# A graph network's prologue: load order, a broadcast by TensorE, sums on other engines, and the moved row counts of later pairs

## The chip, the cores and the metric

The kernel runs on one core of a Trainium2 chip. The metric is the device time of one launch in microseconds (us), the median of several runs. One profiled execution of each kernel gives the spans and traces quoted here. All timed runs that are compared were in the fast state; most experiments were timed once only, with no state on record, so there the traces are compared and not the times. Runs that share a chip are compared with each other first.

## The reference, cut to what matters

128 independent graphs of 128 nodes go through two layers. Layer 0 is graph attention with 8 heads. Layer 1 is two hypergraph convolutions with a layer norm between them.

```python
x, adj: (128, 128, 512), (128, 128, 128)           # float32
# layer 0
feats = einsum('bnf,hfu->bhnu', X, W)              # W: 8 heads, 512 -> 64
dense = leaky_relu(e_self[:, :, :, None] + e_neigh[:, :, None, :], 0.2) + NEG_BIG * (1 - A)
out   = einsum('bhij,bhju->bhiu', softmax(dense), feats) + b
x     = layernorm(x + relu(out))
# layer 1
h = relu(hypergraph_conv(x, adj, W1, b1))          # 512 -> 1024
h = layer_norm(h, gamma, beta)
y = hypergraph_conv(h, adj, W2, b2)                # 1024 -> 512
x = layernorm(x + (y + x))
```

All weights are shared by the graphs. The kernel therefore prepares them once, in its prologue. The layer norm between the two convolutions is folded into W2: each row is scaled by gamma, and a row of weighted means is subtracted (`gw`). A second such row (`bw`) carries beta.

## The kernel before: the parts that matter here

Graphs are handled in 64 pairs, in a software pipeline. Every step of every pair has a number, the list is sorted by it, and the steps are emitted in that order. The numbers order the instructions on each engine; they are no times. The large products with the weights (features, hidden, output) are done by a seven-product scheme, which needs sums of weight blocks (`second_sums`, `prepare_hidden`).

```python
    # first loads: W0 in four blocks on SyncE's queue, then
    as_bc = everywhere(a_self, F, "as_bc")     # everywhere: broadcast load on ScalarE's queue
    an_bc = everywhere(a_neigh, F, "an_bc")
    load(0)                                    # adjacency and its first row, SyncE
    load_blocks(0, nc.scalar)                  # pair 0's x, for the transposes
    load_edges(0, nc.scalar)
    b0_bc = everywhere(b0, F, "b0_bc")
    b2_bc = everywhere(b2, F, "b2_bc")
    for t, ap in ((b1_sb, b1), (gb[:, 0, :], gamma), (gb[:, 1, :], beta)):
        nc.scalar.dma_start(t, ap.rearrange("(k p) -> p k", p=P))
    # ... cut ...
    def nodes(p, s):                           # node degrees of a pair, ends in one small tile
        # ... cut: VectorE, w <- (a != 0) * w with two SBUF inputs ...
        s["dr"] = work.tile([P, B], F32, tag="dr", name=f"dr_{p}")   # a single buffer
        nc.vector.transpose(s["dr"], dn)
    def write_nodes(p, s):
        nc.sync.dma_start(s["dd"].rearrange("b c n -> (b c) n"), s["dr"])
    # ... cut ...
    def prepare_output_sums():                 # pv: the means, made by 32 matmuls
        for j in range(2):
            nc.vector.tensor_copy(sums[:, j * QU:(j + 1) * QU], pv[j][:2, :QU])
        nc.sync.dma_start(sums_d, sums)        # to DRAM ...
        for c, t in ((0, gw), (1, bw_bc)):     # ... and back into all partitions
            nc.sync.dma_start(t, sums_d[c].partition_broadcast(P))
    def prepare_output_blocks(some):           # 16 scalings of W2 by gamma, minus gw
        # ... cut ...
                nc.vector.scalar_tensor_tensor(
                    blk[:, k, :], blk[:, k, :], gb[:, 0, c:c + 1], gw[:, j * QU:(j + 1) * QU],
                    op0=ALU.mult, op1=ALU.subtract,
                )
    # ... cut ...
    first = {                                  # places of the first pairs' steps
        ("nodes", 0): 15.0, ("write_nodes", 0): 16.5, ("spread_nodes", 0): 18.5,
        # ... cut ...
        ("nodes", 1): 17.6, ("write_nodes", 1): 17.9, ("x_transpose", 1): 14.5,
        # ... cut ...
    }
```

Names used below: **pf** is the first layer's feature product, **nb** the neighbour rows on which masks, leaky relu, row maxima (**nm**) and exponentials work, **pav** the attend product, **pv** the means, **pz** the propagate product, **ph** the hidden product in seven parts (accumulators phX, phY, phW), **py** the output product. **y** is a pair's output of the first layer (at L824 of the second), **eT** the transposed exponentials, **dr** the small tile with a pair's node degrees, **ab** its edge blocks. TensorE is called cold where its matmuls take about double the time, warm otherwise.

Of the kernel before, what the change touches and what calls it, by code (L numbers as in the profile page):

```python
# [20 lines left out]
def kernel(  # L21
# [45 lines left out]
    nc = tc.nc  # L67
# [21 lines left out]
    def bank(name):  # L89
        return psum.tile([P, HALF], F32, tag="bank", name=name)  # L90
# [13 lines left out]
    def load_blocks(p, queue=None):  # L104
        s = st[p]
        gs = slice(2 * p, 2 * p + 2)

        s["xb"] = work.tile([P, 2 * NB, P], F32, tag="xb", name=f"xb_{p}")
        rows = x[gs].rearrange("g (b n) (f c) -> f n (g b) c", b=NB, f=NB)
        for f in range(NB):  # L110
            (queue or nc.sync).dma_start(s["xb"][f * B:(f + 1) * B], rows[f])

    def load_edges(p, queue=None):
        s = st[p]

        s["ab"] = work.tile([P, 2 * NB, B], F32, tag="ab", name=f"ab_{p}")
        rows = adj[2 * p:2 * p + 2].rearrange("g (b n) (f e) -> f n (g b) e", b=NB, f=NB)
        for f in range(NB):
            (queue or nc.sync).dma_start(s["ab"][f * B:(f + 1) * B], rows[f])
# [22 lines left out]
    def everywhere(ap, n, name):  # L142
        t = const.tile([P, n], F32, name=name)
        nc.scalar.dma_start(t, ap.partition_broadcast(P))
        return t

    as_bc = everywhere(a_self, F, "as_bc")
    an_bc = everywhere(a_neigh, F, "an_bc")
    load(0)
    load_blocks(0, nc.scalar)  # L150
    load_edges(0, nc.scalar)
    b0_bc = everywhere(b0, F, "b0_bc")
    b2_bc = everywhere(b2, F, "b2_bc")
    bw_bc = const.tile([P, F], F32, name="bw_bc")
# [3 lines left out]
    for t, ap in ((b1_sb, b1), (gb[:, 0, :], gamma), (gb[:, 1, :], beta)):  # L158
        nc.scalar.dma_start(t, ap.rearrange("(k p) -> p k", p=P))
# [28 lines left out]
    def second_sums(w, b12, some=slice(0, 4)):  # L188

        b11, b21, b22, t4, t1, t2, t3 = (w[i] for i in range(7))  # L190
        for dst, in0, in1 in ((t1, b12, b11), (t2, b22, t1), (t3, b22, b12), (t4, b21, t2))[some]:
            nc.vector.tensor_tensor(dst, in0, in1, op=ALU.subtract)
# [13 lines left out]
    def prepare_first_sums():  # L206
        second_sums([w0_sb[:, i] for i in range(7)], w0_12)

    def prepare_hidden(i):
        a11, a12, a22, s1, s2, s3, s4 = (w1_sb[:, i] for i in range(7))  # L210
        dst, in0, in1, op = (
            (s1, w1_21, a22, ALU.add), (s2, s1, a11, ALU.subtract), (s3, a11, w1_21, ALU.subtract),
            (s4, a12, s2, ALU.subtract),
        )[i]
        nc.vector.tensor_tensor(dst, in0, in1, op=op)
# [4 lines left out]
    def prepare_output():  # L220
# [3 lines left out]
        nc.vector.tensor_copy(gbs[:, :, 1], gb[:, 1, :])  # L224
        pv = made["pv"] = [bank(f"pv{j}") for j in range(2)]
# [7 lines left out]
    def prepare_output_sums():  # L233
        pv = made["pv"]
        sums = const.tile([2, F], F32, name="sums")
        for j in range(2):
            nc.vector.tensor_copy(sums[:, j * QU:(j + 1) * QU], pv[j][:2, :QU])
        sums_d = dram.tile([2, F], F32, tag="sums_d", name="sums_d")
        nc.sync.dma_start(sums_d, sums)
        gw = work.tile([P, F], F32, tag="y2", name="gw")  # L240
        for c, t in ((0, gw), (1, bw_bc)):
            nc.sync.dma_start(t, sums_d[c].partition_broadcast(P))
        made["gw"] = gw
# [11 lines left out]
    def prepare_output_block_sums(some):  # L255
        second_sums([w2_sb[:, i, :, :QU] for i in range(7)], w2_12, some)
# [613 lines left out]
    def o_norm(p, s):  # L870
# [9 lines left out]
        (15.8, load_weights, (w2_blocks, w2t, DH // 2, QU)),  # L880
        (16.0, load_weights, (w1_blocks[:2], w1t, F // 2, HALF)),
        (80.2, load_weights, (w1_blocks[2:], w1t, F // 2, HALF)),
        (103.0, prepare_output, ()), (116.5, prepare_output_sums, ()),
        (112.0, prepare_hidden, (0,)), (112.5, prepare_hidden, (1,)),
        (114.5, prepare_hidden, (2,)), (115.0, prepare_hidden, (3,)),
        (122.4, prepare_output_blocks, (slice(0, 2),)),
        (128.4, prepare_output_blocks, (slice(2, 4),)),
        (130.6, prepare_output_block_sums, (slice(0, 2),)),
        (132.8, prepare_output_block_sums, (slice(2, 4),)),
# [4 lines left out]
        ("nodes", 0): 15.0, ("write_nodes", 0): 16.5, ("spread_nodes", 0): 18.5,  # L894
        ("x_transpose", 0): 11.5, ("edges", 0): 15.2, ("scale_edges", 0): 15.4,
        ("spread_rows", 0): 13.5, ("neighbours", 0): 14.0, ("load_rows", 0): 14.2,
        ("propagator", 0): 103.5, ("r_evict", 0): 104.0,
        ("nodes", 1): 17.6, ("write_nodes", 1): 17.9, ("x_transpose", 1): 14.5,
        ("edges", 1): 110.4, ("scale_edges", 1): 110.5,
        ("spread_rows", 1): 79.9, ("neighbours", 1): 80.0,  # L900
        ("propagator", 1): 117.7, ("r_evict", 1): 118.0,
# [10 lines left out]
    for p in range(PAIRS):  # L912
        if p > 1:
            todo.append((p * T, load, (p,)))
            todo.append((p * T + 19.0, load_blocks, (p,)))
            todo.append((p * T + 28.5, load_edges, (p,)))
        for lag, time, name, since, fn, args in steps:
# [11 lines left out]
            todo.append((first.get((name, p), (p + lag) * T + time), run, (fn, p, args)))  # L929
# [46 lines left out]
```

## Time and profile before

| | before |
|---|---|
| median of 3 runs | 2587.31 us (2584.8 to 2587.83) |
| span of the profiled run | 2586.4 us |
| TensorE busy | 2515.8 us |
| TensorE idle before 120 us | 53 us |
| attend of pair 1 begins (the landmark) | 117.71 us |

A line of a timeline gives the start and the length in us, the engine, the source line, the operation with output and inputs, the shapes, and how many instructions were merged. In brackets stands how long the engine had idled before it, and what ended the idling by the profile's account. The lines are in the prediction.

### The profile page before, as it was taken

The numbers are of one execution on the slowest core, as the hardware profiler recorded it, in microseconds if no ns is written. First come the engines' busy times: TensorE is split into PE (matmuls) and PEld (weight loads), VectorE is DVE, ScalarE is ACT, GpSimd is POOL, SyncE is SP. The second block draws the span as 40 slices with busy tenths as digits, with TensorE's granted clock in tenths as the row PEclk, the third lists the DMA queues.
The fourth block names the chain that finished last, engine by engine and source line by source line (L and its number), as shares of the span: only waits on it lengthen the run. The fifth ranks groups of instructions, "written<-read, shape, count | busy, mean of one in ns | idle before, by whom it ended". The sixth has DMA issues, their size and how long they took to land.

```text
span 2586.4 us, 48239 instructions
## 1 busy us (share of the span) xinstructions
PE 2515.8 (97%) x16312; PEld 2274.8 (88%) x16312; DVE 2146.5 (83%) x4650; ACT 1514.4 (59%) x4293; POOL 1714.1 (66%) x1797
## 2 busy tenths in 40 slices
PE   4799999999999999999999999999999999999997
PEld 3699899899999999989899999999989998999996
DVE  4788888888888888888888888888888888888875
ACT  2365565565565565565565665665665665665662
POOL 1567667667667667667667667667667667667753
PEclk8899999999999999999999999999999999999999
DMA  5444444444444444444444444444444444444430
GB/s 146 116 135 132 143 136 132 143 137 132 142 138 132 142 138 132 145 135 132 135 139 137 137 139 136 136 142 134 135 141 137 134 143 135 134 141 137 135 118 33
DMA packets 428250, 345.57 MB, mean 134 GB/s; under 512 B 146658, under 2 KB 377058, under 8 KB 428004
## 3 DMA queue, kind: packets, MB, share of 16 engines
q1 hardware_dynamic: 422132, 340.77, 44.5%
q10 hardware_dynamic: 5872, 1.72, 0.4%
q8 instruction: 130, 2.13, 0.3%
q14 instruction: 116, 0.95, 0.1%
HBM read 240.66 MB, written 101.72 MB: 132 GB/s over the span
## 4 chain that ended last, share of the span: by engine, by line
PE 89%; DMA 4%; DVE 3%; issue 2%; POOL 2%; SPq 0%; ACT 0%; ACTq 0%; POOLq 0%; DVEq 0%
PE phX L725 17%; PE pyX L417 14%; PE phW L725 9%; PE pfX L417 8%; PE pyW L417 8%; PE pav L599 8%; PE phY L725 4%; PE pz L690 4%; PE pq L849 4%; PE pfW L417 4%; PE pyY L417 4%; PE pfY L417 2%; DMA nb<-rd 1%; PE pd L373 1%; DMA dnb<-dd_d 1%
## 5 line engine op out<-in xcount | busy, mean ns | idle before, releaser
L519 POOL TENSOR_TENSOR nb<-nb,neg 128x512 f32<-128x512 f32 x256 | 320.0, 1272 | 117.9 <-DMA nb<-rd 75.0
L725 PEld LDWEIGHTS phX<-zS,w_sb 128*128 128x128 f32 x3072 | 364.8, 193 | 37.5 <-issue 37.5
L293 ACT COPY py<-pyX 128x257 f32<-128x257 f32 (+1 forms) x192 | 71.7, 374 | 548.0 <-PE pyX L417 548.0
L725 PE MATMUL phX<-zS,w_sb 128*128 128x128 f32 x3072 | 376.0, 276 | 7.1 <-issue 7.1
L776 POOL TENSOR_TENSOR sq<-sq 128x512 f32<-128x512 f32 (+2 forms) x384 | 344.9, 898 | 32.4 <-ACT sq L765 11.3
L526 ACT ACTIVATE nb<-nb,ft 128x128 f32<-128x128 f32 x1024 | 325.2, 389 | 50.1 <-POOL nb L519 48.0
L540 ACT ACTIVATE nb<-nb,nm 128x128 f32<-128x128 f32 x1024 | 320.2, 392 | 17.9 <-DVE nm L532 17.9
L646 POOL TENSOR_TENSOR rso<-veo,mhalf 128x2 f32<-128x2 f32 x64 | 44.8, 700 | 344.3 <-DVE veo L644 302.6
L630 DVE SCALAR_TENSOR_TENSOR y<-y,x 128x512 f32<-128x512 f32 x128 | 155.6, 1216 | 137.9 <-POOL y L623 137.9
L599 PEld LDWEIGHTS pav<-ft,eT 128*128 128x128 f32 x2048 | 251.4, 194 | 11.8 <-issue 2.6
L755 ACT ACTIVATE h<-h,b_sb 128x128 f32<-128x128 f32 x768 | 242.1, 392 | 16.9 <-DVE h L740 16.9
L417 PE MATMUL pyX<-w_sb,hS 128*128 128x257 f32 (+1 forms) x1024 | 248.1, 384 | 2.2 <-DVE hS L399 1.8
L599 PE MATMUL pav<-ft,eT 128*128 128x65 f32 x2048 | 246.5, 274 | 2.5 <-DVE eT L561 1.9
L417 PE MATMUL pyW<-w_sb,hS 128*128 128x256 f32 x1024 | 244.1, 380 | 3.7 <-DVE y L808 3.2
L417 PE MATMUL pyX<-w_sb,h 128*128 128x257 f32 (+1 forms) x1024 | 243.2, 379 | 0.0
L623 POOL TENSOR_TENSOR y<-y,b_bc 128x512 f32<-128x512 f32 x128 | 162.1, 1266 | 95.1 <-DVE y L614 95.1
L417 PEld LDWEIGHTS pyW<-w_sb,hS 128*128 128x128 f32 x1024 | 192.1, 189 | 37.2 <-DVE y L808 10.2
L417 PEld LDWEIGHTS pyX<-w_sb,hS 128*128 128x128 f32 x1024 | 190.2, 191 | 28.0 <-issue 2.1
L417 PEld LDWEIGHTS pyX<-w_sb,h 128*128 128x128 f32 x1024 | 189.3, 190 | 24.9
L399 POOL TENSOR_TENSOR xS<-xT 128x256 f32<-128x256 f32 x124 | 117.9, 951 | 89.5 <-DVE xT L337 89.5
L532 DVE TENSOR_REDUCE nm<-nb 128x4 f32<-128x512 f32 x256 | 173.6, 679 | 0.4 <-ACT nb L526 0.4
L293 ACT COPY ph<-phX 128x512 f32<-128x512 f32 x192 | 112.3, 585 | 97.0 <-PE phX L725 93.8
(127 smaller groups left out, 5843.2 us busy)
## 6 DMA issues: line engine op xcount, KB each, us to landing
nb<-rd SPq DMA_DIRECT2D x128, 512.0 KB, 5.9
ed<-nb SPq DMA_DIRECT2D x126, 512.0 KB, 3.2
eb<-ed SPq DMA_DIRECT2D x504, 128.0 KB, 2.9
x<-in_x_dram SPq DMA_DIRECT2D x64, 512.0 KB, 6.9
out_dram<-o SPq DMA_DIRECT2D x64, 512.0 KB, 2.8
xb<-in_x_dram SPq DMA_DIRECT2D x252, 128.0 KB, 3.0
a<-in_adj_dram SPq DMA_DIRECT2D x64, 128.0 KB, 6.1
w<-in_adj_dram SPq DMA_DIRECT2D x128, 64.0 KB, 3.9
```

Source lines behind the costliest of these rows:

```text
L293: nc.scalar.copy(t[:, :n], s[kind, "X"][:, :n])
L417: nc.tensor.matmul(to[:, :n], lhs[:, k, :], rhs[:, k, :n], start=bool(start) and k == 0, stop=(k == nk - 1), skip_group_check=True,)
L519: nc.gpsimd.tensor_tensor(t, t, neg[:, :, None, :].to_broadcast([P, NB, HH, B]), op=ALU.add)
L526: nc.scalar.activation(t, t, AF.Prelu, bias=s["ft"][:, g, h, 0:1], alpha=SLOPE)
L532: nc.vector.tensor_reduce(s["nm"][:, g, hs], scores(p, s, g, hs).rearrange("p b h j -> p h b j"), AX.XY, ALU.max, negate=True,)
L540: nc.scalar.activation(t, t, AF.Exp, bias=s["nm"][:, g, h:h + 1])
L599: nc.tensor.matmul(t[:, h * (U + 1):(h + 1) * (U + 1)], s["eT"][:, g, q * HH + h, :], s["ft"][:, g, q * HH + h, 2:], start=True, stop=True,)
L623: nc.gpsimd.tensor_tensor(s["y"][:, g, :], s["y"][:, g, :], b0_bc, op=ALU.add)
L630: nc.vector.scalar_tensor_tensor(y, y, 0.0, s["x"][:, g, :], op0=ALU.max, op1=ALU.add)
L725: nc.tensor.matmul(to[:, m * N:(m + 1) * N], w[:, k, m * P:(m + 1) * P], rhs[:, k, :], start=bool(start) and m == 0 and k == 0, stop=(k == ...
L755: nc.scalar.activation(dst[:, k, :], src[:, k, :], AF.Relu, bias=b1_sb[:, c:c + 1])
L776: nc.gpsimd.tensor_tensor(t[:, :n, :], t[:, :n, :], t[:, n:2 * n, :], op=ALU.add)
```

## The change

The intent is to shorten the prologue: fewer waits ahead of the first matmul, weights earlier, the means without a trip through DRAM, some sums on GpSimd and ScalarE, and the node counts of later pairs at other places.

```diff
-    as_bc = everywhere(a_self, F, "as_bc")        # b0, b2, b1, gamma, beta follow on ScalarE's queue
-    load(0)
-    load_blocks(0, nc.scalar)
-    load_edges(0, nc.scalar)
+    everywhere(as_bc, a_self, nc.scalar)
+    everywhere(an_bc, a_neigh, nc.scalar)
+    load_blocks(0)                                # on SyncE's queue, ahead of the adjacency
+    load(0)
+    load_edges(0)
+    def load_vectors(some):                       # gamma, beta, b0 / b1, b2: later, on SyncE's queue
 ... cut ...
-            nc.vector.tensor_copy(sums[:, j * QU:(j + 1) * QU], pv[j][:2, :QU])
-        nc.sync.dma_start(sums_d, sums)
-        for c, t in ((0, gw), (1, bw_bc)):
-            nc.sync.dma_start(t, sums_d[c].partition_broadcast(P))
+            nc.scalar.copy(made["sums"][:, j * QU:(j + 1) * QU], made["pv"][j][:2, :QU])
+    def prepare_output_spread():                  # gw and bw stay in PSUM banks
+            nc.tensor.matmul(made[n], made["sel"][:, c, :], made["sums"], start=True, stop=True)
+    def prepare_output_bias():
+        nc.scalar.copy(bw_bc, made["bw"])
 ... cut ...
-        (15.8, load_weights, (w2_blocks, w2t, DH // 2, QU)),
-        (16.0, load_weights, (w1_blocks[:2], w1t, F // 2, HALF)),
-        (80.2, load_weights, (w1_blocks[2:], w1t, F // 2, HALF)),
-        (103.0, prepare_output, ()), (116.5, prepare_output_sums, ()),
+        (15.75, load_vectors, (0,)), (15.8, load_weights, (w1_blocks, w1t, F // 2, HALF)),
+        (16.0, load_weights, (w2_blocks, w2t, DH // 2, QU)), (16.1, load_vectors, (1,)),
+        (79.1, prepare_hidden, (nc.gpsimd, 0)), (79.2, prepare_hidden, (nc.gpsimd, 1)),
+        (80.0, prepare_output_vectors, ()), (98.0, prepare_output, ()),
 ... cut ...
+        (122.0, prepare_output_blocks, (slice(2, 4),)),
+        (126.5, prepare_output_block_sums, (nc.gpsimd, slice(0, 2))),
 ... cut ...
-        ("nodes", 0): 15.0, ("write_nodes", 0): 16.5, ("spread_nodes", 0): 18.5,
+        ("nodes", 0): 14.45, ("write_nodes", 0): 14.5, ("spread_nodes", 0): 15.9,
+        ("attend", 0): 97.85, ("attended", 0): 99.7,           # all four groups ahead of the means
-        ("nodes", 1): 17.6, ("write_nodes", 1): 17.9,
+        ("nodes", 1): 79.92, ("write_nodes", 1): 80.15,
+        ("nodes", 2): 130.0, ("write_nodes", 2): 130.1, ("nodes", 3): 150.0,
```

More of the change, by code (lines that the diff above doesn't have):

```diff
@@ L102, in load, with load_blocks @@
             nc.sync.dma_start(s["w"][:, g, :], adj[2 * p + g, 0, :].partition_broadcast(P))
-    def load_blocks(p, queue=None):
+    def load_blocks(p):
         s = st[p]
@@ L110, in load_blocks, with load_edges @@
         for f in range(NB):
-            (queue or nc.sync).dma_start(s["xb"][f * B:(f + 1) * B], rows[f])
-    def load_edges(p, queue=None):
+            nc.sync.dma_start(s["xb"][f * B:(f + 1) * B], rows[f])
+    def load_edges(p):
         s = st[p]
@@ L118, in load_edges @@
         for f in range(NB):
-            (queue or nc.sync).dma_start(s["ab"][f * B:(f + 1) * B], rows[f])
+            nc.sync.dma_start(s["ab"][f * B:(f + 1) * B], rows[f])
     def block(dst, ap, i, j, rows, cols):
@@ L140, with everywhere @@
         w0_blocks.append((dst, raw.rearrange("p k (h u) -> p k h u", h=HH), j))
-    def everywhere(ap, n, name):
-        t = const.tile([P, n], F32, name=name)
-        nc.scalar.dma_start(t, ap.partition_broadcast(P))
-        return t
-    as_bc = everywhere(a_self, F, "as_bc")
-    an_bc = everywhere(a_neigh, F, "an_bc")
-    load(0)
-    load_blocks(0, nc.scalar)
-    load_edges(0, nc.scalar)
-    b0_bc = everywhere(b0, F, "b0_bc")
-    b2_bc = everywhere(b2, F, "b2_bc")
-    bw_bc = const.tile([P, F], F32, name="bw_bc")
+    def everywhere(t, ap, queue):
+        queue.dma_start(t, ap.partition_broadcast(P))
+    as_bc, an_bc, b0_bc, b2_bc, bw_bc = (
+        const.tile([P, F], F32, name=n) for n in ("as_bc", "an_bc", "b0_bc", "b2_bc", "bw_bc")
+    )
     b1_sb = const.tile([P, KH], F32, name="b1_sb")
     gb = const.tile([P, 2, KH], F32, name="gb")
-    for t, ap in ((b1_sb, b1), (gb[:, 0, :], gamma), (gb[:, 1, :], beta)):
-        nc.scalar.dma_start(t, ap.rearrange("(k p) -> p k", p=P))
+    everywhere(as_bc, a_self, nc.scalar)
[4 more added lines that the diff above has]
+    def load_vectors(some):
+        queue = nc.sync
+        if some == 0:
+            for t, ap in ((gb[:, 0, :], gamma), (gb[:, 1, :], beta)):
+                queue.dma_start(t, ap.rearrange("(k p) -> p k", p=P))
+            everywhere(b0_bc, b0, queue)
+        else:
+            queue.dma_start(b1_sb, b1.rearrange("(k p) -> p k", p=P))
+            everywhere(b2_bc, b2, queue)
     w2_sb = const.tile([P, 7, KH // 2, QU + 1], F32, name="w2_sb")
@@ L186, with second_sums @@
     nc.gpsimd.memset(dn, 0.0)
-    def second_sums(w, b12, some=slice(0, 4)):
+    def second_sums(engine, w, b12, some=slice(0, 4)):
         b11, b21, b22, t4, t1, t2, t3 = (w[i] for i in range(7))
         for dst, in0, in1 in ((t1, b12, b11), (t2, b22, t1), (t3, b22, b12), (t4, b21, t2))[some]:
-            nc.vector.tensor_tensor(dst, in0, in1, op=ALU.subtract)
+            engine.tensor_tensor(dst, in0, in1, op=ALU.subtract)
     def prepare_first(half):
@@ L206, in prepare_first_sums, with prepare_hidden @@
     def prepare_first_sums():
-        second_sums([w0_sb[:, i] for i in range(7)], w0_12)
-    def prepare_hidden(i):
+        second_sums(nc.vector, [w0_sb[:, i] for i in range(7)], w0_12)
+    def prepare_hidden(engine, i):
         a11, a12, a22, s1, s2, s3, s4 = (w1_sb[:, i] for i in range(7))
@@ L214, in prepare_hidden, with prepare_output_vectors, prepare_output @@
         )[i]
-        nc.vector.tensor_tensor(dst, in0, in1, op=op)
+        engine.tensor_tensor(dst, in0, in1, op=op)
     gbs = const.tile([P, KH, 2], F32, name="gbs")
     made = {}
-    def prepare_output():
+    def prepare_output_vectors():
         nc.vector.tensor_scalar(gbs[:, :, 0], gb[:, 0, :], 1.0 / DH, None, op0=ALU.mult)
         nc.vector.tensor_copy(gbs[:, :, 1], gb[:, 1, :])
+        made["sel"] = work.tile([2, 2, P], F32, tag="y2", name="sel")
+        nc.gpsimd.tensor_copy(
+            made["sel"], ident[:2, :2].unsqueeze(2).to_broadcast([2, 2, P])
+        )
+    def prepare_output():
         pv = made["pv"] = [bank(f"pv{j}") for j in range(2)]
@@ L233, in prepare_output_sums @@
     def prepare_output_sums():
-        pv = made["pv"]
-        sums = const.tile([2, F], F32, name="sums")
+        made["sums"] = const.tile([2, F], F32, name="sums")
         for j in range(2):
-            nc.vector.tensor_copy(sums[:, j * QU:(j + 1) * QU], pv[j][:2, :QU])
-        sums_d = dram.tile([2, F], F32, tag="sums_d", name="sums_d")
-        nc.sync.dma_start(sums_d, sums)
-        gw = work.tile([P, F], F32, tag="y2", name="gw")
-        for c, t in ((0, gw), (1, bw_bc)):
-            nc.sync.dma_start(t, sums_d[c].partition_broadcast(P))
-        made["gw"] = gw
+            nc.scalar.copy(made["sums"][:, j * QU:(j + 1) * QU], made["pv"][j][:2, :QU])
+    def prepare_output_spread():
+        made["gw"], made["bw"] = (bank(n) for n in ("gw", "bw"))
+        for c, n in enumerate(("gw", "bw")):
+            nc.tensor.matmul(
+                made[n], made["sel"][:, c, :], made["sums"], start=True, stop=True
+            )
+    def prepare_output_bias():
+        nc.scalar.copy(bw_bc, made["bw"])
     def prepare_output_blocks(some):
@@ L253, in prepare_output_blocks, with prepare_output_block_sums @@
                 )
-    def prepare_output_block_sums(some):
-        second_sums([w2_sb[:, i, :, :QU] for i in range(7)], w2_12, some)
+    def prepare_output_block_sums(engine, some):
+        second_sums(engine, [w2_sb[:, i, :, :QU] for i in range(7)], w2_12, some)
     def prepare_mean_columns():
@@ L879 @@
         (11.8, load_blocks, (1,)), (15.65, load, (1,)), (15.7, load_edges, (1,)),
-        (15.8, load_weights, (w2_blocks, w2t, DH // 2, QU)),
-        (16.0, load_weights, (w1_blocks[:2], w1t, F // 2, HALF)),
-        (80.2, load_weights, (w1_blocks[2:], w1t, F // 2, HALF)),
-        (103.0, prepare_output, ()), (116.5, prepare_output_sums, ()),
-        (112.0, prepare_hidden, (0,)), (112.5, prepare_hidden, (1,)),
-        (114.5, prepare_hidden, (2,)), (115.0, prepare_hidden, (3,)),
-        (122.4, prepare_output_blocks, (slice(0, 2),)),
-        (128.4, prepare_output_blocks, (slice(2, 4),)),
-        (130.6, prepare_output_block_sums, (slice(0, 2),)),
-        (132.8, prepare_output_block_sums, (slice(2, 4),)),
+        (15.75, load_vectors, (0,)), (15.8, load_weights, (w1_blocks, w1t, F // 2, HALF)),
+        (16.0, load_weights, (w2_blocks, w2t, DH // 2, QU)), (16.1, load_vectors, (1,)),
+        (79.1, prepare_hidden, (nc.gpsimd, 0)), (79.2, prepare_hidden, (nc.gpsimd, 1)),
+        (80.0, prepare_output_vectors, ()), (98.0, prepare_output, ()),
+        (112.1, prepare_output_sums, ()), (117.75, prepare_output_spread, ()),
+        (110.6, prepare_hidden, (nc.vector, 2)), (110.7, prepare_hidden, (nc.vector, 3)),
+        (119.85, prepare_output_bias, ()),
+        (117.8, prepare_output_blocks, (slice(0, 1),)),
+        (118.1, prepare_output_blocks, (slice(1, 2),)),
+        (122.0, prepare_output_blocks, (slice(2, 4),)),
+        (126.5, prepare_output_block_sums, (nc.gpsimd, slice(0, 2))),
+        (132.0, prepare_output_block_sums, (nc.vector, slice(2, 4))),
         (100.0, prepare_mean_columns, ()),
@@ L893 @@
     first = {
-        ("nodes", 0): 15.0, ("write_nodes", 0): 16.5, ("spread_nodes", 0): 18.5,
+        ("nodes", 0): 14.45, ("write_nodes", 0): 14.5, ("spread_nodes", 0): 15.9,
         ("x_transpose", 0): 11.5, ("edges", 0): 15.2, ("scale_edges", 0): 15.4,
         ("spread_rows", 0): 13.5, ("neighbours", 0): 14.0, ("load_rows", 0): 14.2,
-        ("propagator", 0): 103.5, ("r_evict", 0): 104.0,
-        ("nodes", 1): 17.6, ("write_nodes", 1): 17.9, ("x_transpose", 1): 14.5,
-        ("edges", 1): 110.4, ("scale_edges", 1): 110.5,
-        ("spread_rows", 1): 79.9, ("neighbours", 1): 80.0,
-        ("propagator", 1): 117.7, ("r_evict", 1): 118.0,
+        ("attend", 0): 97.85, ("attended", 0): 99.7, ("propagator", 0): 97.9, ("r_evict", 0): 100.0,
+        ("nodes", 1): 79.92, ("write_nodes", 1): 80.15, ("x_transpose", 1): 14.4,
+        ("edges", 1): 110.4, ("scale_edges", 1): 110.5, ("spread_nodes", 1): 101.0,
+        ("spread_rows", 1): 79.9, ("neighbours", 1): 80.1,
+        ("propagator", 1): 117.76, ("r_evict", 1): 121.8,
+        ("leaky", 1, 0, 0): 117.85, ("leaky", 1, 0, 1): 117.9, ("leaky", 1, 1, 0): 119.9,
+        ("largest", 1, 0, 0): 118.0, ("largest", 1, 0, 1): 118.2, ("largest", 1, 1, 0): 120.2,
+        ("masked", 1, 0, 0): 109.0,
+        ("nodes", 2): 130.0, ("write_nodes", 2): 130.1, ("nodes", 3): 150.0,
+        ("write_nodes", 3): 150.1, ("skip", 0): 128.5,
     }
@@ L913 @@
         if p > 1:
-            todo.append((p * T, load, (p,)))
+            todo.append(({2: 81.0, 3: 131.0}.get(p, p * T), load, (p,)))
             todo.append((p * T + 19.0, load_blocks, (p,)))
@@ L928 @@
                 }.get((name,) + args[:1], time)
-            todo.append((first.get((name, p), (p + lag) * T + time), run, (fn, p, args)))
+            time += (p + lag) * T
+            todo.append((
+                first.get((name, p) + args, first.get((name, p), time)), run, (fn, p, args)
+            ))
     with tc.manual_schedule():
```

## The prediction

> **What bounds the kernel now.** I read the page's busy shares first. They say TensorE, and the row after it shows VectorE well below.
>
> ```profile
> PE 2515.8 (97%) x16312; PEld 2274.8 (88%) x16312; DVE 2146.5 (83%) x4650; ACT 1514.4 (59%) x4293; POOL 1714.1 (66%) x1797
> ```
>
> The span is 2586.4 us, so TensorE idles only about 70 us in the whole run. Where those 70 us lie decides what a change of the prologue can be worth, so next I asked for the busy time of each engine by stretch of 20 us. The columns are stretch, length, then PE, PEld, DVE, ACT, POOL busy us with counts, granted clock, DMA share, GB/s.
>
> ```profile
> 0.00:20.00 20.00, 0.59 (x1) 0.50 (x2) 9.64 (x14) 2.55 (x4) 6.42 (x15) 1.00 0.84 170
> 20.00:40.00 20.00, 18.08 (x62) 14.42 (x61) 6.39 (x23) 2.82 (x8) 2.45 (x3) 0.91 0.32 96
> 40.00:60.00 20.00, 5.65 (x20) 3.15 (x18) 8.15 (x18) 9.08 (x32) 3.01 (x7) 0.65 0.63 191
> 60.00:80.00 20.00, 15.40 (x68) 8.85 (x68) 6.83 (x24) 1.91 (x4) 3.66 (x3) 0.76 0.57 139
> 80.00:100.00 20.00, 14.03 (x100) 13.84 (x100) 18.66 (x37) 12.05 (x34) 11.75 (x13) 0.75 0.36 100
> 100.00:120.00 20.00, 13.10 (x70) 11.77 (x71) 19.83 (x40) 9.85 (x28) 9.75 (x8) 0.83 0.39 107
> 120.00:140.00 20.00, 20.00 (x119) 17.90 (x119) 15.92 (x35) 9.14 (x25) 15.16 (x16) 1.00 0.37 107
> ```
>
> TensorE idles 53 us before 120 us (120 minus the six PE entries) and not at all from there: from 120 us it is the bound. Before 80 us nobody is busy, so waits decide; from 80 to 120 us VectorE is at 93 to 99% and decides. The instruction order beyond the first pairs is unchanged by the diff. So I need one landmark: the attend matmuls of pair 1, at 117.71 us. Those of the last pair start at 2525.4, which makes 38.8 us a pair over 62 pairs, and 61 us of tail that the change doesn't touch. The new time is the old one minus the shift of that landmark.
>
> Third, the chain of waits in order of time (start, us, what), for what ends late in the prologue:
>
> ```profile
> 1.66 7.94 DMA xb<-in_x_dram
> 9.60 0.02 issue
> 9.62 4.98 DMA xb<-in_x_dram
> ...
> 44.04 8.53 DMA dd_d<-dr
> ...
> 66.22 11.34 issue
> ...
> 95.06 3.63 DMA gw<-sums_d
> ```
>
> Fourth, TensorE's and VectorE's timelines, for who waits there:
>
> ```profile
> 19.41 3.89 PE L454 MATMUL pf<-w_sb,xT 128*128 128x264 f32 x8 [19.41 <-ACT w_sb L196]
> ...
> 65.08 3.58 PE L228 MATMUL pv<-w_sb,gbs 128*2 128x256 f32 x8 [0.89 <-DVE gbs L224]
> ...
> 84.71 3.79 PE L690 MATMUL pz<-R,y 128*128 128x128 f32 x16 [7.91 <-ACT y L667]
> ...
> 105.84 3.76 PE L725 MATMUL phX<-zS,w_sb 128*128 128x128 f32 x16 [7.10 <-issue]
> ```
>
> ```profile
> 52.67 0.21 DVE L318 STREAM_TRANSPOSE dr<-dn 128x32 f32<-128x32 f32 x1 [9.02 <-DMA dd_d<-dr]
> ...
> 98.71 3.07 DVE L250 SCALAR_TENSOR_TENSOR w_sb<-w_sb,gb,gw 128x256 f32<-128x256 f32 x4
> ...
> 107.31 3.25 DVE L250 SCALAR_TENSOR_TENSOR w_sb<-w_sb,gb,gw 128x256 f32<-128x256 f32 x8
> ```
>
> Four holes: the first matmul at 19.41; VectorE shut for 9.02 us because pair 1's node row must wait until pair 0's has left its single buffer, whose store is queued behind weights; 11.34 us in which pair 0's second half waits behind the 32 means matmuls (pv); the round trip of the means through DRAM, with a 7.10 us hole of TensorE after it.
>
> **What the Trainium skill says.** "TensorE: Matmul & The Clock Gate", Part 1: the array runs at half rate until some 3.4 us of sustained work, and falls back after an idle window. The trace agrees: the first 8 pf matmuls take 3.89 us, the last 16 take 3.72, and the granted clock is 0.65 to 0.83 between 40 and 120 us except where work is dense. "DMA: Bandwidth & Descriptors", the anatomy of one DMA: a transfer has a fixed cost of about 2 us whatever its size. Here the 4 KB store of the means took 1.22 us and its 256 KB spread 3.63. "SBUF — State Buffer", Who interferes with whom: a VectorE instruction with two SBUF inputs shares a read port with GpSimd, one with a single SBUF input doesn't. The trace agrees: the four L250 at 98.71, beside GpSimd's xS sums, take 0.77 us each, the eight at 107.31, with GpSimd idle, 0.41. With the means in PSUM this collision should go.
>
> **Part by part**, as a walk along the new order with the durations of the old trace.
>
> 1. Start. Pair 0's x blocks move from ScalarE's queue to SyncE's right behind the first weights, ahead of the adjacency; their last issue waited at 9.62 for an earlier landing and landed at 14.60. As and an, 0.5 MB, first weights, 1 MB, and x, 0.5 MB, are 2 MB, which the DMA had moved by about 10.5 us before; so x is there by 11 and VectorE (its four sums done at 12.4) is the limit: transposes 12.4 to 14.5. ScalarE loses four small loads whose issue held its copies until 17.44. First pf at about 13.5, its 10.3 us done at 23.8 against 29.71: minus 5.9.
> 2. nodes(1) leaves its place ahead of pair 0's row maxima. Means of exponentials then hang on masks alone: neighbour rows land 31.5 (37.4 minus 5.9), masks and leaky until 36.7, 8 exp 39.1, 4 leaky 40.4, 8 exp 42.9. Before: 59.45. Minus 16.5 so far, of which 9 from the wait and the rest from filling.
> 3. All four attend groups ahead of pv. Transposes done at 44, ScalarE's copies at 45.5, 32 attend matmuls about 6.5 us (0.23 us each cold, then 0.11): 51.2. Bias (1.26), residual and statistics (1.6), rstd and shift (1.3), normalisation: pair 0's y at about 58.2 against 84.5. pv takes 32 x 0.222 = 7.1 us warm, and ends at 59 to 60 if W2 has landed; 4.6 MB of weights and vectors issued from 37 at about 280 GB/s (the rate at 42 to 49 us now) are in at 54. So pz starts at 59.5 to 62 against 84.71: minus 23 to 25.
> 4. Means: 6 us of sums copy, store and spread become two ScalarE copies and two 512-column matmuls (pq, of the same shape, takes 0.86). gw is ready some 2.8 us after pz starts, at 62.3 to 65; before, 98.71, 14.0 after pz's start.
> 5. VectorE after that. Removed: two of four hidden sums (2.4), the sums' copies (0.7), two of four output sums (2.4 to 3.4), the other two hidden sums now ahead of gw (3.0), port collisions (1.5). Of 20 us from gw to the landmark's eT some 5 go. But all 16 scalings, an edge count, two x transposes and an h sum now stand ahead of pair 1's last row maximum: about 14 us after gw instead of 5.3. That maximum gates the exponentials, they gate a copy of phX in ScalarE's order, and that gates the fourth-to-last hidden product. This hole of TensorE stays, about 78 to 82, and costs a cold clock: from that product to the landmark was 11.9 us, warm 8.3.
> 6. GpSimd gets four 1024-wide sums, 4 x 2.5 = 10 us. Two stand ahead of the bias (46 to 51, just in time), two ahead of the squares; pair 1's hidden sums aren't needed until 7 us after the landmark. Off the path by my sum, narrowly.
>
> Sum: the product at 78 to 82, plus 8.3 to 11.9, gives the landmark at 86.5 to 94. A walk like this forgets small waits; I take 93, hence minus 24.7: 2587.3 - 24.7 = 2562.6.
>
> **Rivals.** (a) Loads take the place of the waits: W1, W2, gamma and beta stand ahead of pair 1's neighbour rows in one queue; a store behind weights took 8.53 us before. I put those rows at 60; at 66 the masks, leaky and maxima of pair 1 slip and some 5 us come back: 2568. For it: one queue, 4.6 MB. Against: VectorE is still the later of the two. (b) GpSimd becomes the bound: its hidden sums wait for W1 ahead of pair 0's bias, and everything after slips with them, 3 to 8 us: 2566 to 2571. For: GpSimd is in order. Against: W1 is loaded first for that. (c) VectorE's 80 to 118 us block isn't shortened, since what was removed is only 9 of 38 us; then the start of it shifts by 23 and nothing else: 2564. (d) TensorE stays warm and the row maximum isn't late: landmark at 86, 2556. (e) Nothing gained because the prologue is hidden: speaks against it that TensorE has no idle time after 120 us in which to catch up.
>
> **Range and chances.** (a) and (b) together make 2573 to 2576, (d) with a faster load 2552. Range 2552 to 2575. Faster by over 2% needs 51.7 us, that is, all 53 us of TensorE's idle time in the prologue, the 13 us before any input can have arrived included: 0.02. Slower by over 2% would need a lasting stall in each pair, and the order there is unchanged: 0.01.
>
> **What would show it.** First pf near 13.5; no wait of VectorE on dd_d; exponentials done near 43; pz near 60; gw's scalings at 0.4 us each; the phX hole still there, near 80; the landmark near 93 and 38.8 us a pair after it. Wrong if pz starts later than 66 (W1 or W2 late, seen as GpSimd or pv waiting on DMA), if pair 1's neighbour rows land after 66, or if the period per pair changes.

## The result, and the profile after

| | before | after |
|---|---|---|
| median of 6 runs | 2587.4 us (2583.74 to 2589.77) | 2562.57 us (2560.83 to 2565.34) |
| ratio | | 0.9907, 95% interval 0.9894 to 0.992 |
| span of the profiled run | 2586.4 us | 2561.2 us |

A ratio is the mean time of one kernel's fast runs over that of the other's of the same rounds, so not quite the ratio of the medians. The verdict at 2% is "same"; the interval says that the change is faster by 0.8 to 1.1%.

The stretches of 20 us of the changed kernel, with the same columns as before (stretch, length, busy us of PE, PEld, DVE, ACT, POOL with counts, clock, DMA share, GB/s):

```profile
0.00:20.00 20.00, 5.35 (x13) 4.22 (x14) 10.19 (x14) 3.76 (x5) 6.67 (x15) 1.00 0.67 151
20.00:40.00 20.00, 15.88 (x61) 11.82 (x59) 9.80 (x28) 7.10 (x24) 5.31 (x5) 0.91 0.47 112
40.00:60.00 20.00, 18.28 (x77) 12.00 (x76) 10.97 (x34) 5.82 (x19) 8.29 (x9) 0.66 0.77 242
60.00:80.00 20.00, 14.05 (x106) 12.05 (x104) 15.33 (x39) 12.99 (x37) 11.94 (x14) 1.00 0.68 177
80.00:100.00 20.00, 16.65 (x94) 15.54 (x94) 14.98 (x33) 10.52 (x30) 14.57 (x12) 0.83 0.36 95
100.00:120.00 20.00, 18.39 (x119) 16.73 (x119) 16.73 (x43) 10.79 (x31) 12.23 (x14) 1.00 0.43 107
```

The hollow stretch of before, 40 to 60 us with 5.65 us of TensorE, is filled. VectorE's fullest stretch has 16.73 of 20 us where it had been 18.66 and 19.83. Averages over 20 us hide the order in which it works, though: it idles from 69.3 to 72.8 and is busy for 9.33 of the 10.5 us after that. A wait ahead of its work, and not its work alone, now paces it.

TensorE's timeline of the changed kernel, the lines that answer to those of before:

```profile
14.65 3.86 PE L470 MATMUL pf<-w_sb,xT 128*128 128x264 f32 x8 [14.65 <-DVE xT L353]
...
44.31 7.09 PE L615 MATMUL pav<-ft,eT 128*128 128x65 f32 x32 [0.54 <-ACT eT L592]
...
60.75 2.05 PE L706 MATMUL pz<-R,y 128*128 128x128 f32 x16 [0.50 <-ACT y L683]
...
83.35 3.75 PE L741 MATMUL phX<-zS,w_sb 128*128 128x128 f32 x16 [7.01 <-issue]
...
93.74 1.90 PE L615 MATMUL pav<-ft,eT 128*128 128x65 f32 x16
...
111.94 2.00 PE L433 MATMUL pyW<-w_sb,hS 128*128 128x256 f32 x8 [1.61 <-DVE y L824]
```

The first matmul is 4.8 us earlier, pz of pair 0 is 24.0 us earlier, and the landmark is 24.0 us earlier. The hole of 7 us ahead of the hidden product is still there. A new wait of 1.61 us stands at 111.94.

VectorE's timeline of the changed kernel, for what paces that hole and that wait:

```profile
63.89 1.66 DVE L266 SCALAR_TENSOR_TENSOR w_sb<-w_sb,gb,gw 128x256 f32<-128x256 f32 x4
...
72.81 0.45 DVE L366 STREAM_TRANSPOSE hT<-ab 128x256 f32<-128x256 f32 x1 [3.48 <-PE phX L741]
...
80.79 0.68 DVE L548 TENSOR_REDUCE nm<-nb 128x4 f32<-128x512 f32 x1
...
108.61 0.85 DVE L325 SCALAR_TENSOR_TENSOR w<-a,w 128x128 f32<-128x128 f32 x1
...
109.39 1.34 DVE L325 SCALAR_TENSOR_TENSOR w<-a,w 128x128 f32<-128x128 f32 x1
```

The scalings take 0.41 us each. At 72.81 VectorE had idled 3.48 us. The profile blames TensorE's phX, but that instruction had nothing to give to an edge transpose: its input is `ab`, pair 2's edge blocks. Further traces of the same kernel name the load of `ab` there. The last row maximum is done at 81.5, and the hidden product follows 1.9 us later. At 108 us pair 3's node count (L325) takes 0.85 and 1.34 us, where it takes 0.25 to 0.28 for pairs 0 to 2, and TensorE waits for the sum behind it.

Where the edge blocks were, SyncE's queue shows (each line is an issue: start, length of the issue):

```profile
50.26 3.44 SPq L143 DMA_DIRECT2D b_bc<-in_b_dram  x1
53.79 0.38 SPq L499 DMA_DIRECT2D rd<-rows  x1
57.81 0.93 SPq L516 DMA_DIRECT2D nb<-rd  x2
...
66.99 1.91 SPq L119 DMA_DIRECT2D ab<-in_adj_dram  x4
```

The rows of pair 1 had been ready at 44.0 us. Their store was issued at 53.79, landed 3.9 us later, and the edge blocks are issued at 67 because in the one queue they stand behind it, behind the rows' way back (57.81) and behind pair 2's x blocks (issued from 61.70 to 66.37).

One more thing has to be read before small effects are told apart: pz of pair 1 and of the last pair, before and then after.

```profile
136.12 1.95 PE L690 MATMUL pz<-R,y 128*128 128x128 f32 x16
...
2543.15 1.95 PE L690 MATMUL pz<-R,y 128*128 128x128 f32 x16
```

```profile
113.78 1.95 PE L706 MATMUL pz<-R,y 128*128 128x128 f32 x16
...
2517.79 1.95 PE L706 MATMUL pz<-R,y 128*128 128x128 f32 x16
```

The gap between the kernels is 22.3 us at pair 1 and 25.4 us at the last pair. The undisturbed pace is 38.67 us a pair in both, and single pairs take up to 40.3 at scattered places. In these two traces they cost the kernel before 3.0 us more. The orders there are nearly the same, and there is no second trace of before. But in the fourteen traces of this document the same stretch takes 2400.3 to 2407.9 us, in the three of the changed kernel 2403.0 to 2405.6, so 2407.0 against 2404.0 can be chance. Effects of a few us were therefore read at landmarks of the prologue, not from the total.

### The profile page after: what moved, and what is told of

Same layout as the page of the kernel before. It is cut to its first block, busy times and chain, and to the rows that moved or that the text cites. A ratio compares the mean times of both kernels' runs of the same rounds, so it can differ in the third digit from the quotient of the medians.

```text
span 2561.2 us, 48245 instructions
## 1 busy us (share of the span) xinstructions
PE 2513.8 (98%) x16316; PEld 2274.1 (89%) x16316; DVE 2128.5 (83%) x4644; ACT 1516.4 (59%) x4296; POOL 1722.1 (67%) x1802
## 4 chain that ended last, share of the span: by engine, by line
PE 91%; DMA 3%; DVE 2%; issue 1%; POOL 1%; SPq 1%; ACT 0%; POOLq 0%; DVEq 0%
PE phX L741 18%; PE pyX L433 15%; PE phW L741 9%; PE pfX L433 9%; PE pyW L433 8%; PE pav L615 8%; PE phY L741 4%; PE pz L706 4%; PE pfW L433 4%; PE pq L865 4%; PE pyY L433 4%; PE pfY L433 2%; DMA nb<-rd 1%; PE pd L389 1%; DMA rd<-rows 1%
## 5 line engine op out<-in xcount | busy, mean ns | idle before, releaser
L415 POOL TENSOR_TENSOR xS<-xT 128x256 f32<-128x256 f32 x124 | 118.0, 951 | 83.2 <-DVE xT L353 81.5
```

## The experiments

Twelve kernels were run, four in a call, and those of one call share a chip. The landmark is the start of the attend of pair 1. "Theory A" in the expectations says that the landmark follows the chain pair 0's y, means, scalings, row maximum. "Theory B" says that it follows SyncE's queue, by way of pair 2's edge blocks. The last column is the landmark less pz of pair 0. The experiments' single times, 2558.35 (u_nodes) to 2577.36 us (u_store), carry no state and are not compared.

| run (call) | first pf | pair 0's exponentials done | pz of pair 0 | first scaling | hidden product | landmark | pz of pair 1 | pz of pair 0 to landmark |
|---|---|---|---|---|---|---|---|---|
| before | 19.41 | 59.45 | 84.71 | 98.71 | 105.84 | 117.71 | 136.12 | 33.00 |
| after | 14.65 | 43.24 | 60.75 | 63.89 | 83.35 | 93.74 | 113.78 | 32.99 |
| again (1) | 14.94 | 42.53 | 60.66 | 63.80 | 82.62 | 92.48 | 112.72 | 31.82 |
| u_start (1) | 15.63 | 43.82 | 62.63 | 65.77 | 85.24 | 94.86 | 114.90 | 32.23 |
| u_nodes (1) | 14.98 | 44.87 | 61.96 | 65.10 | 81.83 | 92.28 | 112.50 | 30.32 |
| u_pv (1) | 15.08 | 42.58 | 70.88 | 76.70 | 94.51 | 105.14 | 125.31 | 34.26 |
| u_dram (2) | 14.97 | 43.11 | 60.27 | 76.11 | 94.30 | 103.97 | 124.30 | 43.70 |
| u_vec_engine (2) | 15.19 | 44.22 | 60.95 | 64.81 | 83.27 | 95.35 | 116.48 | 34.40 |
| e_vec (2) | 14.89 | 43.86 | 63.13 | 66.28 | 85.60 | 95.31 | 115.25 | 32.18 |
| e_scal (2) | 14.93 | 42.95 | 61.86 | 65.00 | 81.43 | 95.75 | 116.73 | 33.89 |
| u_store (3) | 14.56 | 60.45 | 77.78 | 82.59 | 97.56 | 108.18 | 128.42 | 30.40 |
| e_pool (3) | 15.06 | 44.05 | 61.81 | 66.03 | 81.48 | 91.20 | 111.26 | 29.39 |
| e_best (3) | 14.87 | 42.70 | 60.87 | 64.55 | 77.53 | 89.06 | 107.21 | 28.19 |
| again2 (3) | 14.70 | 43.82 | 62.88 | 66.02 | 84.74 | 94.83 | 114.87 | 31.95 |

**again**: the changed kernel, but for a comment.

> The changed kernel once more, unaltered but for a comment, to see how far the landmarks of a trace repeat. Expected: first pf matmul at 14.65 us, pz of pair 0 at 60.75, attend of pair 1 at 93.74, pz of pair 1 at 113.78, each within 0.5 us (the trace noise that the other runs are read against); span within 2558 to 2565.

Measured: landmark 92.48, span 2559.1, time 2560.9 us. The same kernel in call 3 (again2) had its landmark at 94.83. Three traces of one program thus spread by 2.4 us, a good part of a few of the effects below. My 0.5 us was too tight. Nearly all of the spread, 2.2 us, is there at pz of pair 0 already. In again2 the means matmuls ahead of it had waited for W2; TensorE's timeline of again2:

```profile
53.64 3.57 PE L241 MATMUL pv<-w_sb,gbs 128*2 128x256 f32 x8 [0.71 <-DMA w_sb<-in_w2t_dram]
```

From pz of pair 0 to the landmark the three take 31.82 to 32.99 us. For an edit that acts behind pz this is the better measure.

**u_start**: x and edge blocks of pair 0 back on ScalarE's queue.

```diff
-    load_blocks(0)
     load(0)
-    load_edges(0)
+    load_blocks(0, nc.scalar)
+    load_edges(0, nc.scalar)
```

> The changed kernel with pair 0's x and edge blocks put back on ScalarE's queue, behind the adjacency on SyncE's. Theory A (x landing late is what the start lost): first pf back at 18 to 19.4 us, and everything after it, the queue of loads included, 4 to 5 us later: attend of pair 1 at 97.5 to 98.7. Rival: the first pf hung on ScalarE's copies, which waited for four small vector loads (b0, b2, b1, gamma, beta) in ScalarE's queue; those stay away here, so the first pf would be at 15 to 16.

Measured: first pf at 15.63, against 14.94 in the same call; landmark 94.86 against 92.48. The rival held. Of the 4.8 us that the start gained, the place of x is worth some 0.7; the 2.4 us at the landmark are no more than the spread (again2: 94.83). About 3.8 are left for the other difference at the start: ScalarE no longer issues b0, b2, b1, gamma and beta ahead of its copies of W0. Its first copy begins at 18.73 before and at 13.98 in this run. No run put these loads back alone.

**u_nodes**: pair 1's nodes back ahead of pair 0's row maxima.

```diff
-        ("nodes", 1): 79.92, ("write_nodes", 1): 80.15
+        ("nodes", 1): 17.6, ("write_nodes", 1): 17.9
```

> The changed kernel with pair 1's nodes and their store put back ahead of pair 0's row maxima. Theory of the prediction (the move removes the 9 us wait): VectorE's wait at dr returns with 5 us or more and pair 0's exponentials end at 48 or later. Rival: what removed it is that pair 0's node store now goes ahead of the weights (issued at 29.68, not behind six weight loads), so only about 2.5 us come back, for the load of pair 1's first adjacency row: exponentials done at 45 to 46. Either way theory B says that the attend of pair 1 stays at 93 to 95, because VectorE waits at 69.3 to 72.8 for pair 2's edge blocks, which are late in SyncE's queue.

Measured: exponentials done at 44.87 against 42.53, landmark 92.28 against 92.48. VectorE's timeline of this run:

```profile
35.77 1.27 DVE L325 SCALAR_TENSOR_TENSOR w<-a,w 128x128 f32<-128x128 f32 x1 [5.76 <-DMA w<-in_adj_dram]
```

It waits for pair 1's first adjacency row, over a stretch in which it would have idled 4.5 us anyway. No wait at `dr` is left. The rival held, and the 2.3 us are gone by the landmark: here too VectorE waits (1.76 us) for pair 2's edge blocks.

**u_store**: in addition pair 0's node store behind the weights, as before the change.

```diff
-        ("write_nodes", 0): 14.5, ("spread_nodes", 0): 15.9   # and nodes 1 as in u_nodes
+        ("write_nodes", 0): 16.5, ("spread_nodes", 0): 18.5
```

> The changed kernel with both parts of the node handling put back: pair 1's nodes ahead of pair 0's row maxima, and pair 0's node store behind the weights in SyncE's queue, as before the change. u_nodes put only the first back and cost 2 us there. Theory (the 9 us wait came from the store behind the weights): VectorE's wait at dr is back and longer than before, since 4 MB of weights instead of 3 lie ahead: store issued at 53 to 55, landed at 56 to 60, pair 0's exponentials done at 62 to 68 instead of 43, landmark (attend of pair 1) 108 to 118. Rival (the place of nodes alone made it): as in u_nodes, exponentials at 45, landmark 92 to 95.

Measured: exponentials done at 60.45, landmark 108.18 against 94.83 in the same call. VectorE's timeline of this run:

```profile
53.64 0.21 DVE L334 STREAM_TRANSPOSE dr<-dn 128x32 f32<-128x32 f32 x1 [16.49 <-DMA dd_d<-dr]
```

The wait is back and longer: 16.49 us, with all of W1 and W2 ahead of the store. (The exponentials are still earlier than the 62 to 68 that I expected: the store was issued at 49.56, not at 53 to 55.) So with the nodes in their old place the store's place decides: the exponentials are done at 60.45 here and at 44.87 in u_nodes. Whether moving the nodes alone would do as well no run shows: with the store landing at 53.6 as here, pair 1's row could not have entered `dr` at 45.06, where the changed kernel puts it, and VectorE might have waited there instead.

**u_pv**: the 32 means matmuls back between the two attend halves.

```diff
-        ("attend", 0): 97.85, ... ("propagator", 0): 97.9
+        ("attend", 0): 97.85, ("attend", 0, 1, 0): 98.1, ("attend", 0, 1, 1): 98.2, ... ("propagator", 0): 98.15
```

> The changed kernel with the 32 means matmuls put back between the attend groups of pair 0's two halves. They then wait for W2 (its last part is in at some 56 us), so the second half's attend runs at 58 to 60 and pz of pair 0 goes from 60.75 to 67 to 69. Theory A (VectorE's chain from the means on sets the landmark): attend of pair 1 later by nearly all of that, 98 to 101. Theory B (pair 2's edge blocks at 72.8 set it, with 3.5 us of slack ahead of them): by 1 to 4 us, 95 to 98.

Measured: pz of pair 0 at 70.88, landmark 105.14 against 92.48, 12.7 us later (10.3 against again2). TensorE's timeline of this run:

```profile
70.88 3.78 PE L706 MATMUL pz<-R,y 128*128 128x128 f32 x16 [8.17 <-ACT y L683]
```

Theory A held, and by more than I wrote: y came after an idle time of TensorE of 8.17 us, so pz and the two matmuls for gw ran at 3.78 and 2.07 us instead of 2.05 and 1.12. Theory B's slack is too small to hide this.

**u_dram**: the means through DRAM, on SyncE's queue.

```diff
-            nc.tensor.matmul(made[n], made["sel"][:, c, :], made["sums"], start=True, stop=True)
+        nc.sync.dma_start(made["d"], made["sums"])            # in prepare_output_sums
+        for c, t in ((0, made["gw"]), (1, bw_bc)):
+            nc.sync.dma_start(t, made["d"][c].partition_broadcast(P))
```

> The changed kernel with the means spread through DRAM as before (store and two spreads on SyncE's queue, behind pair 1's x rows as the old order has it) instead of by TensorE. Theory A: the first scaling by the means goes from 63.9 to 75 or later (store not issued before 69.7, some 1.3 us to land, spread 4 to 6 us), and the landmark (attend of pair 1) follows it by 27 to 30 us: 102 to 107. Rival (the load of pair 2's edge blocks sets the landmark and hides the trip): 93 to 96.

Measured: first scaling at 76.11, landmark 103.97. VectorE's timeline of this run:

```profile
76.11 1.67 DVE L262 SCALAR_TENSOR_TENSOR w_sb<-w_sb,gb,gw 128x256 f32<-128x256 f32 x4 [11.54 <-DMA gw<-sums_d]
```

There was no changed kernel in this call; against its three traces elsewhere (92.48 to 94.83) this is 9 to 11.5 us. Theory A held. In the old order the trip took 5.7 us, from the copies of the sums at 92.99 to the first scaling at 98.71. In the new order it takes 15.3, from 60.83 to 76.11: the sums are ready at 61.4, but the store stands behind the loads of pairs 1 and 2 and is issued at 69.21.

**u_vec_engine**: all four moved weight sums back on VectorE.

```diff
-        (79.1, prepare_hidden, (nc.gpsimd, 0)), (79.2, prepare_hidden, (nc.gpsimd, 1)),
+        (110.5, prepare_hidden, (nc.vector, 0)), (110.55, prepare_hidden, (nc.vector, 1)),
-        (126.5, prepare_output_block_sums, (nc.gpsimd, slice(0, 2))),
+        (131.9, prepare_output_block_sums, (nc.vector, slice(0, 2))),
```

> The changed kernel with all hidden and output weight sums back on VectorE, none on GpSimd. VectorE gets 2 x 1.2 us ahead of the scalings and 2 x 1.2 us ahead of pair 1's eT; pair 0's bias on GpSimd no longer stands behind sums that wait for W1, so it is some 3 us earlier, but pz of pair 0 hardly moves (60 to 61) since the means matmuls end at 60.3. Theory (VectorE's 3.5 us wait for pair 2's edge blocks takes up the first part, slack at eT the second): landmark 93 to 95. Rival (VectorE is saturated and every us on it counts): 97 to 99.

Measured: landmark 95.35, 0.5 to 2.9 us later than in the three traces of the changed kernel, pz of pair 1 1.6 to 3.8 later. From pz of pair 0 to the landmark it takes 34.40 us, 1.4 to 2.6 more than they. That is nearer to the theory than to saturation. What "idle engines" brought is small.

**e_vec**: b1 and b2 loaded behind pair 1's x rows.

```diff
-        (16.1, load_vectors, (1,)),
+        (108.5, load_vectors, (1,)),
```

> The changed kernel with the loads of b1 and b2 moved behind pair 1's x rows; they are first used near 83. Theory B (one queue: pair 1's row store waits at 48.2 to 53.8 for the issue of these two): the store is issued at 48 to 49, neighbour rows are there at 60 to 61.5 instead of 62.9, pair 2's edge blocks at 69.5 to 71 instead of 72.8, and the landmark goes to 90 to 92. Rival (the rows wait behind the bytes of W2, not behind the issue): rows at 62 to 63 and the landmark at 92.5 to 94, as it was.

A miss. Measured: the row store is issued at 49.09 as expected, but its 16 KB land only at 58.4, and the neighbour rows are there at 63.4 (63.0 in the first trace of the changed kernel); landmark 95.31, and 32.18 from pz of pair 0, no better than unedited. An earlier issue alone brings nothing. That the store waits behind the bytes of W2, as the rival says, fits this, but no run moved W2.

**e_scal**: the last eight scalings moved into VectorE's wait for the edge blocks.

```diff
-        (122.0, prepare_output_blocks, (slice(2, 4),)),
+        (118.3, prepare_output_blocks, (slice(2, 4),)),
```

> The changed kernel with the last eight scalings moved ahead of pair 2's edge count, into VectorE's wait for the edge blocks. Theory: the 3.2 us of scalings fill the 3 to 3.5 us wait, pair 1's last row maximum is at 76.5 to 78 instead of 80.8, the hidden product that hangs on it at 79.5 to 80.5 instead of 83.35, landmark 89.5 to 91. Rival (GpSimd's sums, or pair 1's first exponentials on ScalarE, are next in line): less than 1.5 us gained, 92 to 93.5.

Measured: the hidden product moved to 81.43 and ran warm (2.02 us), but the landmark was at 95.75, no gain at all. VectorE and then GpSimd of this run:

```profile
81.97 4.52 DVE L694 SCALAR_TENSOR_TENSOR o<-y,b_bc 128x512 f32<-128x512 f32 x2
```

```profile
80.98 2.18 POOL L198 TENSOR_TENSOR w_sb<-w,w_sb 128x1024 f32<-128x1024 f32 x1
83.25 2.69 POOL L198 TENSOR_TENSOR w_sb<-w_sb 128x1024 f32<-128x1024 f32 x1
```

VectorE's skip connection, two instructions with two SBUF inputs each, took 4.52 us beside GpSimd's two big output sums. Behind it the hidden sum was late, then ScalarE, and TensorE idled 5.11 us ahead of the landmark.

**e_pool**: e_scal, and GpSimd's output sums moved ahead of pair 2's x sums.

```diff
-        (126.5, prepare_output_block_sums, (nc.gpsimd, slice(0, 2))),
+        (121.8, prepare_output_block_sums, (nc.gpsimd, slice(0, 2))),
```

> As e_scal, with GpSimd's two output sums moved ahead of pair 2's x sums, so that they run at 73 to 78 beside VectorE's transposes and maxima (one SBUF input) and not at 81 to 86 beside its skip connection (two). Theory (in e_scal VectorE's L694 took 4.52 us for 1.3 to 1.7 and L325 1.35 for 0.28 because GpSimd held the shared port, and that ate the gain): L694 at 1.3 us for the two, and the landmark at 89 to 91, against 95.75 in e_scal and 92.5 to 93.7 in the changed kernel. Rival (something else in ScalarE's or VectorE's order takes it): 92.5 or later.

Measured: the landmark at 91.20, 3.6 us ahead of the changed kernel in the same call (1.1 of them at pz of pair 0 already). VectorE of this run:

```profile
82.01 1.29 DVE L694 SCALAR_TENSOR_TENSOR o<-y,b_bc 128x512 f32<-128x512 f32 x2
```

The same two instructions, starting at nearly the same time, take 1.29 us, now that GpSimd's sums run at 73 to 78. The hidden product stands at 81.43 and 81.48, so the 4.5 us between the two landmarks come after it. The theory held, with the landmark 0.2 us outside its range; the two runs were on different chips.

**e_best** and **again2**: e_pool, with pair 1's last row maximum ahead of pair 2's transposes, and pair 3's nodes behind the sum that TensorE waited for; beside it the changed kernel.

```diff
-        ("masked", 1, 0, 0): 109.0,
-        ("nodes", 2): 130.0, ("write_nodes", 2): 130.1, ("nodes", 3): 150.0, ("write_nodes", 3): 150.1,
+        ("masked", 1, 0, 0): 109.0, ("leaky", 1, 1, 1): 120.42, ("largest", 1, 1, 1): 120.45,
+        ("nodes", 2): 130.0, ("write_nodes", 2): 130.1, ("nodes", 3): 152.0, ("write_nodes", 3): 152.1,
```

> e_pool with pair 1's last row maximum moved ahead of pair 2's x transposes, and pair 3's nodes moved behind y_sum. Expected: hidden product at 77.5 to 79.5, landmark at 87 to 89.5, the 1.6 to 1.8 us wait of TensorE for y ahead of the last pyW gone, so pz of pair 1 at 105.5 to 108.5 against 112.7 to 113.8: 5 to 8 us faster than the changed kernel, 2555 to 2558. Rival (VectorE's block is saturated, so an earlier maximum moves the hole only): landmark 90 to 91.5 and 3 us.

> The changed kernel itself, timed on the same chip beside e_best: 2562 to 2563, ratio to before 0.990 to 0.991.

Measured, all in the fast state on one chip: e_best 2560.57 us (2559.43 to 2564.05, 4 runs), the changed kernel 2566.22 (2563.65 to 2567.5, 5 runs), the kernel before 2586.6 (2584.72 to 2588.2, 9 runs). The ratios to before are 0.9901 (0.9888 to 0.9915) and 0.992 (0.9907 to 0.9934). These intervals overlap; the runs themselves hardly do. The trace is clearer. TensorE's timeline of e_best:

```profile
77.53 2.02 PE L741 MATMUL phX<-zS,w_sb 128*128 128x128 f32 x16 [1.76 <-issue]
...
107.21 1.95 PE L706 MATMUL pz<-R,y 128*128 128x128 f32 x16
```

The hole of 7 us is 1.76, the landmark is 5.8 us and pz of pair 1 is 7.7 us ahead of again2, and no wait stands ahead of pyW any more. Of both figures 2.0 us are there at pz of pair 0, ahead of all that was edited, so the edits are worth some 3.8 and 5.7 us. A wait of 2.70 us ahead of the landmark is left. The times that I expected, 2555 to 2558 and 2562 to 2563, and the changed kernel's ratio of 0.990 to 0.991 were missed: the changed kernel itself was 3.7 us slower here than in the result. Whether the chip makes that is not shown.

## Why the prediction was right, point by point

The total was right to 0.1 us (2562.6 against 2562.57). To be that close is luck: the fast runs alone span 4.5 us, and errors of the steps cancelled.

1. **Start.** Predicted 13.5, measured 14.65 (to 14.94): x landed at 13.33, not 11. The step named two causes; u_start shows that x's place is the small one; by subtraction ScalarE's loads are the large one.
2. **The wait at dr.** The time was right (42.9 against 43.24). The reason wasn't: "nodes(1) leaves its place" is not what the 9 us hung on alone. u_nodes put it back and the wait didn't return; u_store shows that the store ahead of the weights is enough. The prediction's rival list didn't have this.
3. **Attend ahead of pv.** Right: y somewhat late (first half normalised from 59.88), pv done at 60.24, pz at 60.75 in the range of 59.5 to 62. u_pv confirms the step and gives it 10.3 to 12.7 us.
4. **Means.** Right: scalings began at 63.89, in the range of 62.3 to 65 for gw. u_dram gives the step 9 to 11.5 us.
5. **VectorE after that.** The scalings' 0.41 us and the remaining hole were right, the product's time wasn't: 83.35, outside "78 to 82". The term that was missing is the 3.48 us wait for pair 2's edge blocks. Rival (a) said of the loads that "VectorE is still the later of the two". That step failed: from 69.3 to 72.8 the loads were the later. Pair 1's neighbour rows, put at 60, came at 62.9. u_nodes, with first scalings 1.3 us later and the same landmark, shows this slack; u_pv and u_dram, with 12 us, go through it. The "some 5" us that should go between gw and the landmark's eT did not go: from the first scaling to that transpose it took 18.2 us before and 26.2 after. From product to landmark it was 10.39, inside 8.3 to 11.9.
6. **GpSimd.** Right that it was narrow: its first sums waited for W1 until 47.99 and held pair 0's bias until 53.17. pv ended at 60.24 and pz waited 0.50 us more for y, so the hold cost at most that. Not foreseen for the new order: GpSimd's sums and masks stretch VectorE's two-input instructions. In the changed kernel the stretched L325 at 108.61 ran beside GpSimd's masks (106.81 to 110.60), and TensorE lost 1.61 us at 111.94; in e_scal it ate a whole gain.

The landmark came out at 93.74 against 93. But the table shows one thing that the walk and its sum hide: from pz of pair 0 to the landmark it took 33.00 us before and 32.99 after. All 24 us stand at pz already. The means came 10.9 us nearer to pz, and the stretch from the first scaling to the landmark grew by as much. That is what rival (c) said: the start of VectorE's block shifts and nothing else, 2564. The runs of the result, 2560.8 to 2565.3, can't tell it from 2562.6; u_dram shows that the means can't go back in the new order, not that they shortened this stretch.

After the landmark the prediction assumed equal pace and lost nothing; in the traces the wait at pyW cost 1.6 us and scattered slow pairs gave 3.0 back.

The parts don't add up to the whole. Undone one at a time u_pv, u_dram and u_store cost 12.7, some 10 and 13.4 us, which is more than the 24 us gained. Each old form is worse in the new order than it was in the old one: the wait at `dr` is 16.49 us against 9.02, from exponentials to pz it takes 28.3 against 25.3, from pz to the first scaling 15.8 against 14.0. More weights stand ahead of the store, and more loads ahead of the means.

## What to carry to other kernels

A small store or load in an in-order DMA queue costs what stands ahead of it (16.49 us of waiting in u_store), so place the small ones that something waits for ahead of the large ones that nothing needs yet. Work put on an engine that idles can still slow its neighbour: move it to a stretch in which the neighbour's instructions don't share its port, and look at the duration of the same instruction before and after (4.52 us in e_scal, 1.29 in e_pool). An effect of a few microseconds is read at a landmark of the trace, with the same kernel traced again beside it, not from the total.

## What the Trainium skill lacked or had wrong

- "SBUF — State Buffer", Who interferes with whom: it says that a VectorE instruction with two SBUF inputs contends with a GpSimd instruction that reads SBUF. The runs agree, and in this case it has this size: two 128x512 instructions took 4.52 us beside GpSimd's 128x1024 sums, and 1.29 us without them. The scalings with one input in PSUM stayed at 0.41 us each, with GpSimd at work beside them (63.03 to 68.80).
- "DMA: Bandwidth & Descriptors", the anatomy of one DMA: its fixed cost of about 2 us is stated for the path by way of GpSimd, and is no guide to SyncE's queue, which all these transfers took. There the 4 KB of means took 1.22 us before the change, and 16 KB issued at 49.09, behind the weights, landed at 58.4 in e_vec. I found no figure on the page for a small transfer with megabytes ahead of it in its queue.
- "TensorE: Matmul & The Clock Gate", Part 1: nothing found wrong in its fall to half rate after an idle window. After 7.01 us of idling the 16 hidden matmuls took 3.75 us, after 1.76 us of idling 2.02.
